# Window attention and a Fourier convolution on one core: the first rows' order, an earlier residual load, one block of transposes and a DMA queue in program order

## The chip, the cores and the metric

The kernel runs on one core of a Trainium2 chip. The metric is the device time of one execution in microseconds (us). Five engines matter: TensorE (PE, its weight loads PEld), VectorE (DVE), ScalarE (ACT), GpSimd (POOL) and SyncE (SP), which here does nothing but issue DMAs, one after the other, each with its waits.

## The reference

The input is x, 32 images of 56 x 56 tokens with 128 channels, in float32. Two residual layers follow each other:

```python
x = x + window_attention(group_norm(x))
x = x + fourier_feedforward(group_norm(x))
```

The group norm takes 32 groups of four channels over a whole image. The attention shifts the image by three, cuts it into 64 windows of 7 x 7 tokens, computes q, k and v, adds a relative position bias and a shift mask to the scores, takes the softmax of four heads, multiplies by v and projects. The second layer takes a cosine transform along the width and one along the height, keeps 32 modes of each, multiplies each mode by its own 128 x 128 matrix, transforms back, adds the two results, and applies `relu(h @ W1 + b1) @ W2 + b2` with 512 hidden channels.

## The kernel before

**Rows and cycles.** An image is worked on in eight rows of eight windows. The loop at L1006 runs over cycles; a cycle begins one row of attention and carries older work along: row `cycle` of attention gets q, k, scores and v, row `cycle - 2` (or in even cycles rows `cycle - 2` and `cycle - 1`) is transposed, row `cycle - 3` gets its product with v and its projection, and the sums for the second group norm follow a cycle later. The convolution of an image follows 11 cycles behind its attention, in steps c = 0 to 15: c = 0 the transform along the width (L645 with `dct_w`), c = 1 and 2 the one along the height (L645 with `dct_h`, from token columns "htok" that are read back from DRAM), c = 3 to 5 the mode products (`mix`, L679), which are written to DRAM ("zscr", L689), c = 5 to 8 the transform back (L718, from "zT", read from DRAM at L700), and in c = 8, 9, 10, 12, 13, 14, 15 seven groups of tokens of the feed-forward part. So a cycle of a middle image does a row of attention, a step of the convolution of the image before and often a group of the feed-forward part of the one before that.

**The order.** On PE, ACT, DVE and POOL instructions run in the order in which the Python code emits them: the whole loop stands under `manual_schedule` with these four engines (L999). SP isn't among them: the scheduler places the DMAs in its queue. Cycles 0 to 10 have no convolution and go through `first_rows` (L956); later ones go through `halves_first` (L850), `eighths`, `quarters`, `full` (L906) and `halves_last` (L927). In the last cycles, where no attention is left, a shorter sequence at L1011 to L1018 is used, which ends with `last_out`, `quarters` and `load_back`.

**PSUM.** Two sets of four banks: "pa" (`attn_bank`) for attention, "pc" (`conv_bank`) for the convolution and the feed-forward part. A bank is given out anew when its reader has finished.

**The next image.** `image_begin` (L256) starts the load of the next image's tokens "xl" in row 3, its second half follows in row 4 (`next_begin`, L947). `image_groups` (L267) turns two rows of it: fourteen transposes (L275) of a full 112 x 128 array into two banks, three copies by ACT for each pair of rows (L287, L288, L293), one `bn_stats` by DVE for each row (L297), and by POOL a memset for each row and the addition of the projection's bias to xl (L306). It is called twice in row 5 and twice in row 6; for image 1 twice in row 4 and twice in row 5 (`next_groups`, L916). Row 6 is an even cycle, and there the calls follow the attention's own transposes L474. `image_norm` (L315) then makes from the statistics the group norm's reciprocal root (L355), the scaled weights "wn" on ACT (L362), "nb" on DVE (L359) and with one small matmul of nb (L112) the bias of v, in steps that a `next(norm)` starts one by one.

**The feed-forward part.** `ff_in` (L738) first loads the residual tokens "res" (L744, L748) from DRAM, adds b2 to them on POOL (L751), and then does the four L112 products with relu on ACT (L763). `ff_out` (L766) does the second product, adds res on DVE (L787) and writes the result (L799 to L807). "res" has two buffers.

**The start.** `bias_and_mask` (L187) fills the sum of position bias and mask with sixteen small DVE additions (L193) for each of two kinds of rows; the second kind is filled in cycle 1. The second group norm's statistics come from `attn_sums` (L557): two DVE sums (L561, L570) and a square on ACT (L569), and from `fourier_stats` (L579), which ends in a reciprocal root on POOL (L616).

Of the kernel before, what the change touches and what calls it, by code (L numbers as in the profile page):

```python
# [15 lines left out]
P = 128  # L16
# [19 lines left out]
JP = 64  # L36
# [12 lines left out]
def swin_fourier_kernel(  # L49
# [33 lines left out]
    def attn_bank():  # L83
        return bank("pa", 4)

    def conv_bank():
        return bank("pc", 4)
# [96 lines left out]
    nc.gpsimd.memset(bm, 0.0)  # L184
    rpb_f = rpb.rearrange("p (t u) y x -> p t u (y x)", u=2)

    def bias_and_mask(r):  # L187
        for t in range(2):
            for half in range(2):
                rows = slice(half * JP, half * JP + WT)  # L190
                for k, p0, p1 in ((0, 0, NP - half), (1, NP - half, NP)):
                    for p in range(p0, p1):
                        nc.vector.tensor_tensor(  # L193
                            bm[rows, r, t, p],
                            rpb_f[rows, t],
                            mask_sb[rows, r, k].unsqueeze(1).to_broadcast([WT, 2, WT]),
                            ALU.add,
                        )

    bias_and_mask(0)  # L200
    dct_w = const_load([TC, 2 * NM], dct, "dct_w")
    dct_h = const.tile([TC, 2 * NM], F32, tag="dct_h", name="dct_h")
    for r in range(0, TC, S):
# [63 lines left out]
    def image_groups(im, i):  # L267


        pt = [attn_bank(), attn_bank()]  # L270
        pts = [
            p[:, : n * S].rearrange("p (j r s) -> p j r s", r=n, s=WS) for p, n in zip(pt, (8, 6))
        ]
        for c in range(7):
            nc.tensor.transpose(  # L275
                pts[c // 4][:, :, 2 * (c % 4) : 2 * (c % 4) + 2],
                im.x[:, WS * i // 2 + c],
                ident_x[:, :, SS:].rearrange("p r (j s) -> p j r s", s=WS),
            )
        for k in range(2):  # L280

            im.xw[i + k] = big.tile([P, RT + JP - WT], F32, tag="xw", name="xw", bufs=10)
            nc.gpsimd.memset(im.xw[i + k][:, RT:], 0.0)
            xw = im.xw[i + k][:, :RT]
            dst = xw.rearrange("p (j r s) -> p j r s", r=WS, s=WS)
            if k:
                nc.scalar.copy(dst[:, :, 0], pts[0][:, :, WS])  # L287
                nc.scalar.copy(  # L288
                    dst[:, :, 1:].rearrange("p j r s -> p j (r s)"),
                    pts[1].rearrange("p j r s -> p j (r s)"),  # L290
                )
            else:
                nc.scalar.copy(  # L293
                    dst.rearrange("p j r s -> p j (r s)"),
                    pts[0][:, :, :WS].rearrange("p j r s -> p j (r s)"),
                )
            nc.vector.bn_stats(im.st[:, i + k], xw)  # L297
        if im.b:
            image_bias(im, i)
# [15 lines left out]
    def image_norm(im):  # L315
# [38 lines left out]
        rstd = small.tile([P, 1], F32, tag="rstd0", name="rstd0")  # L354
        nc.gpsimd.tensor_tensor(rstd, ve, mhalf, ALU.pow)  # L355
        im.w = work.tile([P, 3 * C], F32, tag="wn", name="wn")
        yield
        nb = small.tile([P, 1], F32, tag="nb0", name="nb0")
        nc.vector.scalar_tensor_tensor(  # L359
# [3 lines left out]
        yield  # L363
        pb = attn_bank()
        halved(pb[:, 0:1], wqkv[:, 2 * C :], nb)
        im.bias = small.tile([P, 5], F32, tag="bqkv", name="bqkv")
        nc.vector.tensor_copy(im.bias[:, 2:3], pb[:, 0:1])
        yield

# [83 lines left out]
    def attn_exp(r):  # L453
        a3 = a_sb[r % 3].rearrange("p t w j -> p (t w) j")[:, :, 0:WT]
        nc.scalar.activation(a3, a3, AF.Exp)  # L455
# [279 lines left out]

    def ff_in(im, g):  # L738
        t0, n = sum(FF_GROUPS[:g]), FF_GROUPS[g]
        k, last = n // P, n % P  # L740
        xff = im.xf.rearrange("p r w -> p (r w)")
        scr_tok = im.scr.rearrange("h w c -> (h w) c")
        res = work.tile([P, 4, C], F32, tag="res", name="res")
        nc.sync.dma_start(  # L744
            res[:, :k], scr_tok[t0 : t0 + k * P].rearrange("(n p) c -> p n c", p=P)
        )
        if last:
            nc.sync.dma_start(res[:last, k], scr_tok[t0 + k * P : t0 + n])  # L748
        for c0, c1, m in ((0, k, P), (k, k + 1, last)):
            if m:  # L750
                nc.gpsimd.tensor_tensor(  # L751
                    res[:m, c0:c1],
                    res[:m, c0:c1],
                    b2sb[:m].unsqueeze(1).to_broadcast([m, c1 - c0, C]),
                    ALU.add,
                )
        im.res = res
        im.hid = []
        for f in range(NF):
            ph = conv_bank()  # L760
            halved(ph[:, :n], wff1[:, f * P : (f + 1) * P], xff[:, t0 : t0 + n])
            hf = work.tile([P, HB], F32, tag="hid", name="hid", bufs=NF)
            nc.scalar.activation(hf[:, :n], ph[:, :n], AF.Relu, bias=b1sb[:, f : f + 1])  # L763
            im.hid.append(hf)

    def ff_out(im, g):  # L766
        t0, n = sum(FF_GROUPS[:g]), FF_GROUPS[g]
# [67 lines left out]
    def load_back(cycle):  # L835
        for im, c in fourier(cycle):
            for width, g in back_groups(c):
                load_modes(im, width, g)

    def nothing():  # L840
        while True:
            yield
# [7 lines left out]
    def halves_first(cycle, norm):  # L850
# [8 lines left out]
        im, i = row(cycle)  # L859
        if im:  # L860
            attn_qk(im, i, False)
        next(norm)
        next(sums)
        for im, c in fourier(cycle):
            if c in FF_AT:
# [1 line left out]
        for im, c in fourier(cycle):  # L867
            if c == 0:
                next(im.stats)

    def has_ff(cycle):
        return any(c in FF_AT for _, c in fourier(cycle))
# [43 lines left out]
    def next_groups(cycle):  # L916
        b, i = divmod(cycle, NWR)
        if b + 1 < NB:
            for j in {(4 if b == 0 else 5): (0, 2), (5 if b == 0 else 6): (4, 6)}.get(i, ()):
                image_groups(images[b + 1], j)  # L920

    def last_out(cycle):
# [4 lines left out]
    def halves_last(cycle, norm):  # L927
# [6 lines left out]
        load_back(cycle + 1)  # L934
        next_begin(cycle)
        load_first(cycle)
        next(norm)
        if row(cycle)[0]:
            attn_exp(cycle)
            attn_divide(cycle)  # L940
# [1 line left out]
        if im:  # L942
            last_out(cycle)
            attn_project(im, j)
        next(norm)

    def next_begin(cycle):  # L947
        b, i = divmod(cycle, NWR)
# [7 lines left out]
    def first_rows(cycle, norm):  # L956
# [15 lines left out]
            attn_max(cycle)  # L972
        if im3:
            attn_project(im3, i3)
        next(norm)
        last, j = row(cycle - 4)
        if last:
            for _ in attn_sums(last, j):
# [2 lines left out]
            attn_v(im, i, cycle)  # L981
        if cycle < NWR // 2:
            image_bias(im, 2 * cycle)
        if cycle == 1:
            bias_and_mask(1)
        next(norm)
        next_begin(cycle)
        next_groups(cycle)
        if cycle == CONV_BEGIN - 1:
            attn_exp(cycle)  # L990
            attn_divide(cycle)
            for _ in attn_sums(im3, i3):
                pass
            last, j = row(cycle - 1)
            attn_transpose(last, j, cycle - 1)
        next(norm)

    ET = mybir.EngineType
    with tc.manual_schedule(engines={ET.PE, ET.Activation, ET.DVE, ET.Pool}):  # L999
        images[0] = image_begin(0)  # L1000
        for i in range(0, NWR, 2):
            image_groups(images[0], i)
        for _ in image_norm(images[0]):
            pass
        norm = nothing()
        for cycle in range(NB * NWR + CONV_BEGIN + FF_AT[-1] - NWR + 1):  # L1006
            if cycle < CONV_BEGIN:
                first_rows(cycle, norm)
# [16 lines left out]
                full(cycle)  # L1025
                halves_last(cycle, norm)
            b, i = divmod(cycle, NWR)
            norm = nothing()
            if i == (NWR - 2 if b else NWR - 3) and b + 1 < NB:
                norm = image_norm(images[b + 1])  # L1030
                next(norm)


# [60 lines left out]
```

## Time and profile before

| | |
|---|---|
| time, median of three runs | 3634.03 us (3633.53 to 3636.36) |
| profiled execution | 3641.7 us, span 3639.9 us |
| granted TensorE clock, mean | 0.995 |
| instructions | 161,666 |
| DMA | 390.31 MB, 107 GB/s on average |

Three groups of the profile's fifth part show the largest shares of TensorE: L112 from "hid" (12,544 matmuls of 128 x 128, 740.3 us), L112 from "xf" (3,584 matmuls, 717.5 us) and L112 from "xw" (2,048 matmuls, 390.6 us). The transposes L275 are 896 of 72,192 matmuls. How to read it: each line of that part is a group of equal instructions with its engine, source line, what it writes and reads, count, busy time, mean duration and the idle time of its engine just before it. A "128*64" is the part of the array that a matmul uses. L112 is a helper that splits every product into two halves of 64 columns, so that line is told apart by its tiles. The waits, the timeline and the stretches shown below are answers of the same trace.

### The profile page before, as it was taken

Reading aid. Unit: us, or ns where it says so; the run is one execution under the profiler, and the core shown is the slowest. Engines: PE = TensorE matmul, PEld = TensorE weight load, DVE = VectorE, ACT = ScalarE, POOL = GpSimd, SP = SyncE. Lnnn points to the kernel's source line nnn. Section 1 sums busy time; section 2 is a strip of 40 time slices with the busy share of each in tenths; the row PEclk is TensorE's granted clock in tenths of the full one; section 3 lists DMA queues with packets and bytes.
Section 4 is the critical chain, followed back from the end, with each engine's and each line's share of the span. In section 5 each row is a group of like instructions: output and inputs, shape, how many; then the busy total and the mean of one; then the engine's idle time right before and its main releaser. Section 6 shows DMA issues by size and latency. Waiting matters only on the chain.

```text
span 3639.9 us, 161666 instructions
## 1 busy us (share of the span) xinstructions
PE 3574.4 (98%) x72192; PEld 2832.6 (78%) x72192; DVE 2211.9 (61%) x4738; ACT 2148.1 (59%) x4044; POOL 1368.3 (38%) x1421
## 2 busy tenths in 40 slices
PE   7899999999999999999999999999999999999999
PEld 5677777778777787877777878777777777787776
DVE  7766666666666666666656656666566666565641
ACT  4555566655566555666556665556665556655553
POOL 5433333333343433333333434333333334343321
PEclk8999999999999999999999999999999999999999
DMA  4334434444434444334444344443444443444343
GB/s 114 86 102 112 113 96 111 108 110 111 112 97 112 112 109 116 94 110 107 113 108 111 94 114 109 113 114 94 111 108 111 110 111 94 114 109 109 97 115 98
DMA packets 687350, 390.31 MB, mean 107 GB/s; under 512 B 39967, under 2 KB 657600, under 8 KB 686400
## 3 DMA queue, kind: packets, MB, share of 16 engines
q1 hardware_dynamic: 686045, 379.65, 38.3%
q8 instruction: 568, 9.31, 1.1%
q14 instruction: 126, 1.03, 0.1%
q10 hardware_dynamic: 611, 0.32, 0.0%
HBM read 218.29 MB, written 161.48 MB: 104 GB/s over the span
## 4 chain that ended last, share of the span: by engine, by line
PE 92%; DVE 4%; issue 1%; ACT 1%; POOL 1%; DMA 1%; SPq 0%; POOLq 0%; DVEq 0%; ACTq 0%
PE pc L112 37%; PE pa L112 14%; PE pa L408 6%; PE pc L679 6%; PE pa L474 6%; PE pc L645 6%; PE pa L430 5%; PE pa L499 4%; PE pc L718 4%; PE pa L275 3%; DVE a L438 1%; DVE xf L729 0%; DVE oT L530 0%; POOL rstd L616 0%; ACT a L455 0%
## 5 line engine op out<-in xcount | busy, mean ns | idle before, releaser
L449 POOL TENSOR_TENSOR a<-a,mx 128x784 f32<-128x784 f32 x256 | 389.4, 1521 | 1427.3 <-DVE mx L448 1203.4
L112 PE MATMUL pc<-wff,hid 128*64 128x128 f32 x12544 | 740.3, 273 | 1.5 <-ACT hid L763 0.8
L112 PE MATMUL pc<-xf,wff 128*64 128x512 f32 (+2 forms) x3584 | 717.5, 539 | 1.1 <-DVE xf L729 1.0
L112 PEld LDWEIGHTS pc<-wff,hid 128*64 128x64 f32 x12544 | 702.6, 137 | 8.2 <-ACT hid L763 4.5
L460 DVE TENSOR_REDUCE sm<-a 128x16 f32<-128x784 f32 x256 | 248.2, 970 | 686.1 <-ACT a L455 682.8
L463 POOL TENSOR_TENSOR a<-a,rs 128x784 f32<-128x784 f32 x256 | 389.1, 1520 | 566.6 <-DVE rs L462 542.8
L763 ACT ACTIVATE hid<-pc,b1sb 128x512 f32<-128x512 f32 (+2 forms) x896 | 527.1, 632 | 76.6 <-PE pc L112 74.5
L112 PEld LDWEIGHTS pc<-xf,wff 128*64 128x64 f32 x3584 | 279.8, 137 | 368.0 <-issue 260.5
L379 ACT ACTIVATE q<-pa,bqkv 128x392 f32<-128x392 f32 x256 | 150.4, 587 | 473.1 <-PE pa L112 467.5
L112 PE MATMUL pa<-xw,wn 128*64 128x392 f32 (+1 forms) x2048 | 390.6, 497 | 3.7 <-DVE aT L484 2.7
L530 DVE TENSOR_SCALAR oT<-pa,bqkv 128x98 f32<-128x98 f32 (+2 forms) x768 | 171.0, 278 | 268.7 <-PE pa L499 268.6
L751 POOL TENSOR_TENSOR res<-res,b2sb 128x512 f32<-128x512 f32 (+2 forms) x256 | 264.2, 1037 | 113.5 <-DMA res<-scr 113.5
L408 PE MATMUL pa<-wn,xw 128*64 128x128 f32 x4096 | 283.6, 280 | 4.7 <-issue 3.5
L306 POOL TENSOR_TENSOR xl<-xl,bproj 112x512 f32<-112x512 f32 (+1 forms) x256 | 286.8, 1142 | 0.0
L499 PEld LDWEIGHTS pa<-aT,v 49*32 49x32 f32 x16384 | 172.9, 106 | 146.1 <-issue 127.0
L415 ACT COPY v<-pa 128x512 f32<-128x512 f32 x256 | 150.9, 589 | 228.3 <-PE pa L408 228.3
L438 DVE TENSOR_TENSOR a<-pa,bm 128x392 f32<-128x392 f32 x512 | 264.8, 559 | 25.8 <-PE pa L430 2.1
L455 ACT ACTIVATE a<-a 128x784 f32<-128x784 f32 x256 | 222.3, 869 | 97.2 <-POOL a L449 96.8
L482 ACT COPY aT<-pa 113x452 f32<-113x452 f32 x256 | 139.4, 544 | 210.4 <-PE pa L474 206.6
L408 PEld LDWEIGHTS pa<-wn,xw 128*64 128x64 f32 x4096 | 221.4, 137 | 38.6 <-issue 9.1
L112 PE MATMUL pa<-wproj,oT 128*64 128x128 f32 (+1 forms) x3584 | 248.0, 274 | 1.8 <-DVE oT L530 1.8
L448 DVE TENSOR_REDUCE mx<-a 128x16 f32<-128x784 f32 x256 | 246.3, 962 | 4.3
(91 smaller groups left out, 5583.8 us busy)
## 6 DMA issues: line engine op xcount, KB each, us to landing
zscr<-z SPq DMA_DIRECT2D x512, 112.0 KB
htok<-scr SPq DMA_DIRECT2D x256, 196.0 KB
zT<-zscr SPq DMA_DIRECT2D x192, 256.0 KB
res<-scr SPq DMA_DIRECT2D x160, 256.0 KB
out_dram<-res SPq DMA_DIRECT2D x160, 256.0 KB
scr<-xl SPq DMA_DIRECT2D x128, 224.0 KB
xl<-in_x_dram SPq DMA_DIRECT2D x32, 784.0 KB
xl<-in_x_dram SPq DMA_DIRECT2D x32, 672.0 KB
```

The lines of the kernel that those rows point to most:

```text
L112: nc.tensor.matmul(dst[ps], lhsT=lhsT[:, ps], rhs=rhs, start=start, stop=stop)
L306: nc.gpsimd.tensor_tensor(piece, piece, bproj.unsqueeze(1).to_broadcast([TC, e - a, C]), ALU.add)
L408: nc.tensor.matmul(pv[hs, j * C : (j + 1) * C], lhsT=im.xw[i][:, w * WT : w * WT + JP], rhs=im.w[:, 2 * C : 3 * C], start=True, stop=True,)
L438: nc.vector.tensor_tensor(a[:, 2 * hp : 2 * hp + 2, :, 0:WT].rearrange("p u w j -> p w u j"), ps[hp][:, :RT].rearrange("p (w u j) -> p w u ...
L448: nc.vector.tensor_reduce(mx, a3, axis=AX.X, op=ALU.max)
L449: nc.gpsimd.tensor_tensor(a3, a3, mx.unsqueeze(2).to_broadcast([P, 2 * NWR, WT]), ALU.subtract)
L455: nc.scalar.activation(a3, a3, AF.Exp)
L460: nc.vector.tensor_reduce(sm, a3, axis=AX.X, op=ALU.add)
L463: nc.gpsimd.tensor_tensor(a3, a3, rs.unsqueeze(2).to_broadcast([P, 2 * NWR, WT]), ALU.mult)
L499: nc.tensor.matmul(po4[u][h * HD : (h + 1) * HD, 2 * f + e], lhsT=v[ks, 2 * f + e, h * HD : (h + 1) * HD], rhs=im.aT[i][f][ks, h, e * JP : ...
L751: nc.gpsimd.tensor_tensor(res[:m, c0:c1], res[:m, c0:c1], b2sb[:m].unsqueeze(1).to_broadcast([m, c1 - c0, C]), ALU.add,)
L763: nc.scalar.activation(hf[:, :n], ph[:, :n], AF.Relu, bias=b1sb[:, f : f + 1])
```

## The change

It has these parts:

- `bias_and_mask` is cut into four parts of four L193 each; for the second kind of rows part 0 is emitted in cycle 1, part 1 in cycle 2, parts 2 and 3 in cycle 3, instead of all in cycle 1.
- `image_groups` takes "pc" banks for rows 2 and 6, "pa" banks for rows 0 and 4; from the second image on all four calls stand in row 6, instead of two in row 5 and two in row 6.
- The norm of image 0 runs three steps ahead of the loop, and its last step (the matmul of nb) after the first scores. That of image 1 does its statistics in cycle 6 and the rest in cycle 7, instead of all in cycle 6.
- In cycle 10 the sums of row 7 stand ahead of the exponential and the division of the last row.
- The residual is loaded by `load_residual` at the end of the cycle before, after that cycle's `load_modes`; the addition of b2 on POOL stands after the feed-forward products and after `fourier_stats`.
- SP is added to the engines of `manual_schedule`.

```diff
-    def bias_and_mask(r):
-        for t in range(2):
-            for half in range(2):
...
+    def bias_and_mask(r, part):
+
+        t, half = divmod(part, 2)
...
-        pt = [attn_bank(), attn_bank()]
+
+        pt = [conv_bank() if i % 4 else attn_bank() for _ in range(2)]
...
-    def ff_in(im, g):
+    def load_residual(im, g):
...
+        im.next_res = res
...
+    def ff_residual(im, g):
...
             for width, g in back_groups(c):
                 load_modes(im, width, g)
+            if c in FF_AT:
+                load_residual(im, FF_AT.index(c))
...
         for im, c in fourier(cycle):
             if c == 0:
                 next(im.stats)
+        for im, c in fourier(cycle):
+            if c in FF_AT:
+                ff_residual(im, FF_AT.index(c))
...
-            for j in {(4 if b == 0 else 5): (0, 2), (5 if b == 0 else 6): (4, 6)}.get(i, ()):
+            for j in ({4: (0, 2), 5: (4, 6)} if b == 0 else {6: (0, 2, 4, 6)}).get(i, ()):
...
-        if cycle == 1:
-            bias_and_mask(1)
-        next(norm)
+        for part in {1: (0,), 2: (1,), 3: (2, 3)}.get(cycle, ()):
+            bias_and_mask(1, part)
+        if cycle == NWR - 1:
+            next(norm, None)
         next_begin(cycle)
         next_groups(cycle)
         if cycle == CONV_BEGIN - 1:
+            for _ in attn_sums(im3, i3):
+                pass
             attn_exp(cycle)
             attn_divide(cycle)
-            for _ in attn_sums(im3, i3):
-                pass
...
-        next(norm)
...
-    with tc.manual_schedule(engines={ET.PE, ET.Activation, ET.DVE, ET.Pool}):
+    with tc.manual_schedule(engines={ET.PE, ET.Activation, ET.DVE, ET.Pool, ET.SP}):
...
-        for _ in image_norm(images[0]):
-            pass
-        norm = nothing()
+        norm = image_norm(images[0])
+        for _ in range(3):
+            next(norm)
```

On each engine the same instructions are issued as before, in another order; half of the L275 transposes write to the other set of banks. In the built SP queue, against the one of before, a middle image shows these moves: the first half of the next image's xl stands ahead of the first four htok loads instead of behind them, and the second half comes a cycle later; the zT loads of L718's first and second cycles stand behind the zscr writes of the same cycle instead of ahead of them; every residual load stands near the end of the cycle before its use, instead of wherever the scheduler put it. At the very end the last residual load stands behind the last but one group's output instead of ahead of it.

## The prediction

> **What bounds the kernel now.** I read the page first: the busy line, the 40 slices and the chain that ended last.
>
> ```profile
> PE 3574.4 (98%) x72192; PEld 2832.6 (78%) x72192; DVE 2211.9 (61%) x4738; ACT 2148.1 (59%) x4044; POOL 1368.3 (38%) x1421
> ...
> PE   7899999999999999999999999999999999999999
> ...
> PE 92%; DVE 4%; issue 1%; ACT 1%; POOL 1%; DMA 1%; SPq 0%; POOLq 0%; DVEq 0%; ACTq 0%
> ```
>
> TensorE is busy 98% and holds 92% of the chain; only its first slices are below nine tenths. An edit off TensorE can therefore pay only in the first 200 us or at the end; elsewhere it must shorten TensorE's own sequence. The stretches say the same (busy time of PE, PEld, DVE, ACT, POOL; granted clock; DMA share; GB/s):
>
> ```profile
> 40.00:72.00 32.00, 30.35 (x587) 22.96 (x589) 27.34 (x57) 20.03 (x42) 26.63 (x29) 0.89 0.71 222
> 72.00:84.00 12.00, 7.59 (x126) 5.07 (x126) 7.14 (x23) 5.12 (x9) 2.64 (x3) 0.67 0.08 20
> ...
> 1000.00:1110.70 110.70, 110.51 (x2258) 88.36 (x2257) 68.77 (x148) 66.83 (x126) 42.60 (x44) 1.00 0.40 109
> ```
>
> An image in the middle costs 110.70 us with 0.2 us of visible idling; 72 to 84 us is half empty and at two thirds of the clock. Then the timeline of TensorE around the next image's transposes (start, length, line), first in an odd cycle, then in the even one after it, and from the waits what stops the second (total, times, longest):
>
> ```profile
> 1013.39 0.91 PE L430 MATMUL pa<-k,q 64*64 64x98 f32 x32
> 1014.23 1.72 PE L275 MATMUL pa<-ident_x,xl 112*128 112x112 f32 x14
> 1015.88 1.09 PE L408 MATMUL pa<-wn,xw 128*64 128x128 f32 x16
> ...
> 1027.33 1.85 PE L474 MATMUL pa<-ident,a 113*113 113x113 f32 x16
> 1029.01 1.98 PE L275 MATMUL pa<-ident_x,xl 112*128 112x112 f32 x14
> 1030.92 1.09 PE L408 MATMUL pa<-wn,xw 128*64 128x128 f32 x16
> ```
>
> ```profile
> PEld pa L275 <- DVE aT L484: 7.6, 29, 0.3
> ```
>
> From first start to the next line's start, the odd block takes 1.65 us and the even one 1.91 us. The even one stops once for 0.3 us, because its second pair of "pa" banks is the pair that L484 still copies from. Last, the start-up's DVE and TensorE, and SP's queue:
>
> ```profile
> 33.69 6.23 DVE L193 TENSOR_TENSOR bm<-rpb,mask 49x98 f32<-49x98 f32 x16
> ...
> 77.12 0.38 PE L112 MATMUL pa<-nb,wqkv 128*64 128x1 f32 x4 [4.41 <-DVE nb L359]
> ...
> 1055.17 1.13 SPq L700 DMA_DIRECT2D zT<-zscr  x2
> 1060.18 1.63 SPq L689 DMA_DIRECT2D zscr<-z  x4
> ...
> 1093.94 1.79 SPq L667 DMA_DIRECT2D htok<-scr  x4
> 1099.54 2.00 SPq L118 DMA_DIRECT2D xl<-in_x_dram  x2
> ```
>
> **What the Trainium skill says.** "TensorEngine Tiling (Array Packing)", section Key Properties: changing the tiling mode drains TensorE. The trace agrees: inside a block the transposes start 0.102 us apart, but the first takes 0.156 and the last, before the 64-column L408, 0.192. "TensorE: Matmul & The Clock Gate", What's actually happening: an idle window of about 3.4 us halves the clock. It agrees: after the 4.41 us wait the eight L112 matmuls of cycle 7 take 2.8 us, against 1.4 us in cycle 8. "SBUF — State Buffer", Who interferes with whom: a DVE instruction with two SBUF inputs is blocked by a GpSimd one that reads SBUF. It agrees: L193 has two, takes 0.25 us alone, but three of the sixteen took 1.57, 1.32 and 0.97 us beside L449 and L306. "DMA: Bandwidth & Descriptors", Queues, rings and completion order: an engine consumes its descriptors in ring order, so a load waits out what was queued ahead of it; this trace has only consistent cases.
>
> **The change, part by part** (minus is time saved).
>
> *One transpose block.* The same 28 transposes are issued per image, all in the cycle after L474. The odd block's 1.65 us goes; 14 more transposes cost 14 x 0.102 = 1.43. So one entry and one exit go (0.05 + 0.09), and with them the 0.3 us wait: between the first pair of "pa" banks and the second now stand seven transposes (0.7 us) into "pc", so L484 is done. I take one extra bank-change step of 0.055: 1.65 + 1.43 + 0.055 = 3.14 against 1.65 + 1.91 = 3.56. Saved 0.41 an image, between 0.25 (a 0.15 us bank wait stays) and 0.52. Images 3 to 31 are TensorE-bound: 29 x 0.41 = **-11.9** (-7 to -15). What comes with the block hides. ACT's twelve copies take about 0.9 us a group, so its row is 3.6 us long, and it idles 40%. DVE's eight L297 end before the row's exp does. POOL gets eight L306 (8 x 1.14 = 9.1 us) ahead of L463, which then ends some 5 us later, but its reader L474 comes over a cycle (13 us) later; behind it wait L355 and L751, whose readers also have a cycle.
>
> *Norm of image 1 over cycles 6 and 7.* TensorE no longer waits for nb. DVE then paces: its L460 rows are 13.2 us apart (69.58 to 82.79) over that wait, and 8.0 in the half-clock cycle after it, against 6.5 in undisturbed cycles. The norm's own DVE work is 2.6 + 0.3. Saved (13.2 + 8.0) - (2 x 6.5 + 2.9) = 5.3, and 0.2 for the missing wake-up: **-5.5** (-4 to -6.5).
>
> *Bias of L193 in thirds.* Four now stand ahead of L484 instead of sixteen; the fourth ended at 36.84, the last at 39.92, so 3.1 us earlier. The other twelve move behind L448 and L547 of cycles 2 and 3, beside L449 and the two L306, where each POOL instruction blocks one: about 1.8 and 2.3 us given back, as DVE paces those cycles. **+1** (-2 to +3).
>
> *Sums ahead of exp in cycle 10.* They fill 1.08 us in which DVE waits for L455, less the wait for the square: **-0.6** (-1.2 to 0). *nb's matmul after the first scores, eight banks for image 0:* 0, since L112 waits for wn (ready 18.38) and the second half of the transposes for its DMA (10.5).
>
> *SP in program order.* (a) The next image's xl goes ahead of htok. In a middle image SP stands at xl until L645 ends and issues it at 1099.54, as now; htok, and behind it out and scr, come after; 784 + 784 KB at 233 KB/us (191 GB/s at a DMA share of 0.82 in 1104 to 1112 us) plus 1.7 us of latency (res, 128 KB: issued 3630.07, used 3632.32) lands near 1108; L645 needs it at 1112.6: 0. In image 0 nothing stands before L645: xl at 118.8, htok's first group lands near 125.5, needed at 123.1, and the second group adds a little; the cycle has a 2.1 us wait of its own behind it. **+2.5** (0 to +3.5). (b) zT for L718's second cycle goes from 1055.2 to behind L689 and the residual: issued until 1063.5, landed by 1063.5 + 1.7 + 384/233 = 1066.9, needed at 1069.6: 0. That for its first cycle lands 4 us early, the later two are held by the zT buffers as now. (c) The residual a cycle ahead waits for an out DMA issued a cycle before: 0. POOL's reciprocal root L616 stands before L751 now; no middle image waited on it: 0. (d) At the end the last residual goes behind the last but one out DMA (3632.96 + 0.49): issued 3633.5, added by 3636.5, where L787 now starts at 3635.73: **+0.8** (0 to +1.5).
>
> Sum: -11.9 - 5.5 + 1 - 0.6 + 2.5 + 0.8 = -13.7. The span of the profiled execution, 3639.9, would become 3626.2. The three timed runs stand at 3633.5 to 3636.4, median 3634.03, 5.9 under that span; the same cut gives **3620 us**.
>
> **The rivals.** *R1, the blocks don't pack:* every seven transposes wait for a bank and 28 cost what two blocks cost. For it: each block shows one or two 0.156 steps. Against it: eight banks are in turn, and ACT frees a group in 0.9 us. 3620 + 12 = 3632. *R2, the irregular waits change:* images 3 to 30 take 111.24 us on average against the smallest 110.70, together 15 us, most of it ended by "issue" at L408, L718 and L645 while DMA bursts run. The new order spreads xl's second half to a later cycle; half of it gone is 3612, all 3605; half as much again is 3628. *R3, slower:* L718's second cycle waits for zT each image, since it is now queued behind 448 KB of L689 and 160 KB of residual. The gain is used up when it lands 0.5 us after 1069.6, that is 6.6 us after its last issue, where I count 3.4; a forecast of slower by 0.2% needs 0.7 us after; 1 us an image gives 3620 + 29 = 3649. Against it: the DMA engines are 23% busy from 1059 to 1065. That the change doesn't do what it says can't be: the built order shows one block of 28.
>
> **How the numbers follow.** My forecast 0.58 (alone 3612 to 3629: ends of the start-up terms and of the block), R1 0.12, R2 down 0.14, R2 up 0.08, R3 0.08. Within 0.2% (7.3 us, about what this kernel's measurement can tell from no change) lie most of R1, half of R2 up and the upper tail of the forecast: 0.20; slower is R3, 0.08; faster the rest, 0.72. The range 3606 to 3634 leaves out R3 and the far ends.
>
> **What would show it.** One L275 group of 28 of about 3.14 us between L474 and L408, and L430 to L408 directly in the odd cycle; a smallest image of 110.3; no wait on nb near 77 us; a wait at L645 near 123 us; L787 at the end waiting for the residual. Wrong if the image period stays at 110.7, if L718 waits at its second cycle, or if the start-up, measured to the first middle image, isn't shorter by 1 to 5 us.

## The result, and the profile after

The changed kernel takes 3654.23 us (median of four runs, 3651.56 to 3654.81), the kernel before, in runs beside it, 3635.2 us (median of four, 3633.53 to 3639.87). The ratio is 1.0049, with a 95% interval of 1.0031 to 1.0066: slower by about 19 us between the medians, where 3620 was predicted, with 3634 as the upper end of the range. The profiled execution of the changed kernel took 3651.56 us, its span is 3649.7 us, 9.8 more than the span before (3639.9).

Lines of the changed file stand a little lower, and those of the runs differ again by a few. Here L408 is now L410, L430 L432, L474 L476, L275 L277, L438 L440, L448 L450, L530 L532, L645 L647, L718 L720, L729 (the transform's sum into xf on DVE) L731, L616 and L618 (root and shift) L618 and L620, L359 (nb) L362, L787 L798, and the residual's addition on POOL, L751, is L770.

From the page, the busy line, TensorE's slices and the chain that ended last:

```profile
PE 3557.7 (97%) x72192; PEld 2824.6 (77%) x72192; DVE 2291.8 (63%) x4738; ACT 2146.0 (59%) x4044; POOL 1370.7 (38%) x1421
...
PE   6899999999999999999999999999999999999999
...
PE 82%; DVE 10%; issue 3%; POOL 3%; ACT 1%; DMA 1%; SPq 0%; POOLq 0%; DVEq 0%; ACTq 0%
```

TensorE's busy time fell by 16.7 us, as a shorter block of transposes should make it. But its share of the chain fell from 92% to 82%, and DVE's went from 4% to 10%: something on DVE now sets the time again and again. DVE itself is busy 80 us longer with the same work, so some of its instructions take longer. The three stretches are two in the start and one image in the middle. Their columns are length, busy time of PE, PEld, DVE, ACT and POOL, granted clock, DMA share and GB/s:

```profile
40.00:72.00 32.00, 26.65 (x536) 20.33 (x536) 31.05 (x60) 19.25 (x41) 24.16 (x28) 0.89 0.62 202
72.00:84.00 12.00, 8.91 (x200) 6.85 (x200) 11.21 (x30) 6.18 (x12) 6.67 (x6) 1.00 0.08 21
1000.00:1111.18 111.18, 110.17 (x2258) 87.88 (x2256) 71.39 (x148) 66.83 (x126) 42.63 (x45) 1.00 0.41 108
```

A middle image takes 111.18 us, 0.48 more than before, and DVE is busy 2.6 us more in it. TensorE's timeline around the transposes (start, length, line) shows that this isn't their doing:

```profile
1031.95 0.91 PE L432 MATMUL pa<-k,q 64*64 64x98 f32 x32
1032.78 1.85 PE L476 MATMUL pa<-ident,a 113*113 113x113 f32 x16
1034.47 0.93 PE L277 MATMUL pa<-ident_x,xl 112*128 112x112 f32 x7
1035.23 0.88 PE L277 MATMUL pc<-ident_x,xl 112*128 112x112 f32 x7
1035.94 0.87 PE L277 MATMUL pa<-ident_x,xl 112*128 112x112 f32 x7
1036.65 0.87 PE L277 MATMUL pc<-ident_x,xl 112*128 112x112 f32 x7
1037.46 1.09 PE L410 MATMUL pa<-wn,xw 128*64 128x128 f32 x16
```

From the first start to L410 the 28 transposes take 2.99 us, where 3.14 was predicted and 3.56 stood before. So 0.57 us an image were won there, and as the image is 0.49 longer, about 1.06 were lost elsewhere. The waits of TensorE from 300 to 3600 us (total, times, longest) show where, first in the kernel after, then in the one before:

```profile
PE pc L647 <- DVE xf L731: 30.9, 29, 1.2
```

```profile
PE pc L645 <- DVE xf L729: 0.2, 1, 0.2
```

Once in each of 29 images the first transform along the width waits for DVE's sum into xf. The timeline of POOL, DVE and TensorE around one of these waits, in the kernel after (start, length):

```profile
1099.60 0.55 POOL L618 TENSOR_TENSOR rstd<-ve,mhalf 128x1 f32<-128x1 f32 x1 [3.04 <-DVE ve L614]
1100.11 1.27 POOL L770 TENSOR_TENSOR res<-res,b2sb 128x512 f32<-128x512 f32 x1
...
1100.18 1.22 DVE L620 SCALAR_TENSOR_TENSOR shift<-ms,rstd 128x1 f32<-128x1 f32 x1 [0.66 <-POOL rstd L618]
1101.32 0.66 DVE L532 TENSOR_SCALAR oT<-pa,bqkv 128x98 f32<-128x98 f32 x3
1101.90 1.02 DVE L440 TENSOR_TENSOR a<-pa,bm 128x392 f32<-128x392 f32 x2
1102.85 1.73 DVE L731 TENSOR_TENSOR xf<-pc,xf 128x448 f32<-128x448 f32 x4
...
1103.51 1.21 PE L647 MATMUL pc<-dct_w,xl 112*64 112x64 f32 x34 [1.01 <-DVE xf L731]
```

And the same place in the kernel before:

```profile
1093.07 0.55 POOL L616 TENSOR_TENSOR rstd<-ve,mhalf 128x1 f32<-128x1 f32 x1 [1.81 <-DVE ve L612]
...
1093.65 0.16 DVE L618 SCALAR_TENSOR_TENSOR shift<-ms,rstd 128x1 f32<-128x1 f32 x1 [0.66 <-POOL rstd L616]
1093.72 0.67 DVE L530 TENSOR_SCALAR oT<-pa,bqkv 128x98 f32<-128x98 f32 x3
1094.31 1.03 DVE L438 TENSOR_TENSOR a<-pa,bm 128x392 f32<-128x392 f32 x2
1095.25 1.74 DVE L729 TENSOR_TENSOR xf<-pc,xf 128x448 f32<-128x448 f32 x4
```

The shift, one number per partition, takes 1.22 us instead of 0.16 and ends with the residual's addition, which POOL began 0.07 us before it. Everything behind it on DVE comes 1.06 us later, and L647 reuses a "pc" bank that L731 empties. In the trace after, 31 of the 32 shifts start while L770 runs, and those take 1.216 to 1.232 us; the one of the first image, which has no feed-forward part beside it, takes 0.159. In the kernel before, L751 ran from 1089.97 to 1091.25, 2.4 us ahead of the shift; 31 of its 32 shifts take 0.16 us, and only the last image's, which meets an addition, takes 1.27.

The start also went another way than predicted: forecast 2.6 us shorter in all, it became 3.5 longer. TensorE's and DVE's timelines after:

```profile
85.00 0.38 PE L112 MATMUL pa<-nb,wqkv 128*64 128x1 f32 x4 [2.83 <-DVE nb L362]
85.21 2.89 PE L112 MATMUL pa<-xw,wn 128*64 128x393 f32 x8
...
126.20 3.25 PE L647 MATMUL pc<-dct_h,htok 112*64 112x64 f32 x56 [4.20 <-DMA htok<-scr]
...
34.26 3.15 DVE L193 TENSOR_TENSOR bm<-rpb,mask 49x98 f32<-49x98 f32 x4
41.11 3.97 DVE L193 TENSOR_TENSOR bm<-rpb,mask 49x98 f32<-49x98 f32 x4
50.01 4.58 DVE L193 TENSOR_TENSOR bm<-rpb,mask 49x98 f32<-49x98 f32 x8
```

The wait on nb is still there, only later. L647 waits 4.20 us for htok; that wait was foreseen. The sixteen L193 take 11.7 us, where 6.23 stood before. The start is counted up to the middle images, that is to v's product (L410) of the fourth image's first row, "image 3" in the prediction, which counts from 0. It is 285.1 us, against 281.6 before.

An image's time is counted from its first v's product to that of the next image. The shortest of 27 such times is called the smallest image, and what the 27 take together above 27 times the smallest are the irregular waits. The sum over the two traces is then: start +3.5; 27 images at 0.49 more in the smallest, +13.3; irregular waits 15.2 before and 6.4 after, -8.8; the rows of the last two images +1.4; from the last row's L410 to the end +0.5. That is +9.9, of the 9.8 in the spans.

### The profile page after: what moved, and what is told of

It reads as the page before. It is cut to its first block, busy times and chain, and to the rows that moved or that the text cites. A ratio compares the mean times of both kernels' runs of the same rounds, so it can differ in the third digit from the quotient of the medians.

```text
span 3649.7 us, 161663 instructions
## 1 busy us (share of the span) xinstructions
PE 3557.7 (97%) x72192; PEld 2824.6 (77%) x72192; DVE 2291.8 (63%) x4738; ACT 2146.0 (59%) x4044; POOL 1370.7 (38%) x1421
## 4 chain that ended last, share of the span: by engine, by line
PE 82%; DVE 10%; issue 3%; POOL 3%; ACT 1%; DMA 1%; SPq 0%; POOLq 0%; DVEq 0%; ACTq 0%
PE pc L112 33%; PE pa L112 12%; PE pc L681 6%; PE pc L647 6%; PE pa L410 5%; PE pa L432 5%; PE pa L476 5%; PE pa L501 4%; PE pc L720 3%; DVE xf L731 2%; DVE a L440 2%; POOL a L451 1%; PE pa L277 1%; PE pc L277 1%; POOL a L465 1%
## 5 line engine op out<-in xcount | busy, mean ns | idle before, releaser
L451 POOL TENSOR_TENSOR a<-a,mx 128x784 f32<-128x784 f32 x256 | 389.4, 1521 | 1281.1 <-DVE mx L450 879.8
L465 POOL TENSOR_TENSOR a<-a,rs 128x784 f32<-128x784 f32 x256 | 389.1, 1520 | 613.9 <-DVE rs L464 537.3
L770 POOL TENSOR_TENSOR res<-res,b2sb 128x512 f32<-128x512 f32 (+2 forms) x256 | 264.0, 1036 | 220.1 <-DMA res<-scr 172.8
L532 DVE TENSOR_SCALAR oT<-pa,bqkv 128x98 f32<-128x98 f32 (+2 forms) x768 | 170.9, 277 | 252.6 <-PE pa L501 252.4
L410 PE MATMUL pa<-wn,xw 128*64 128x128 f32 x4096 | 284.2, 280 | 4.7 <-issue 2.2
L308 POOL TENSOR_TENSOR xl<-xl,bproj 112x512 f32<-112x512 f32 (+1 forms) x256 | 287.0, 1143 | 0.0
L440 DVE TENSOR_TENSOR a<-pa,bm 128x392 f32<-128x392 f32 x512 | 264.8, 559 | 24.9 <-PE pa L432 0.8
L798 DVE TENSOR_TENSOR res<-pc,res 128x512 f32<-128x512 f32 (+3 forms) x257 | 139.2, 550 | 180.2 <-PE pc L112 136.5
L432 PE MATMUL pa<-k,q 64*64 64x98 f32 x8192 | 235.9, 251 | 15.4 <-DVE k L398 5.7
L410 PEld LDWEIGHTS pa<-wn,xw 128*64 128x64 f32 x4096 | 221.9, 137 | 37.5 <-issue 4.1
```

The source lines that it names most:

```text
L308: nc.gpsimd.tensor_tensor(piece, piece, bproj.unsqueeze(1).to_broadcast([TC, e - a, C]), ALU.add)
L410: nc.tensor.matmul(pv[hs, j * C : (j + 1) * C], lhsT=im.xw[i][:, w * WT : w * WT + JP], rhs=im.w[:, 2 * C : 3 * C], start=True, stop=True,)
L432: nc.tensor.matmul(ps[hp][HALVES[e], pr * 2 * WT : (pr + 1) * 2 * WT], lhsT=q[cs, w * WT : w * WT + JP], rhs=k_sb[cs, :, w], start=True, s ...
L440: nc.vector.tensor_tensor(a[:, 2 * hp : 2 * hp + 2, :, 0:WT].rearrange("p u w j -> p w u j"), ps[hp][:, :RT].rearrange("p (w u j) -> p w u ...
L451: nc.gpsimd.tensor_tensor(a3, a3, mx.unsqueeze(2).to_broadcast([P, 2 * NWR, WT]), ALU.subtract)
L465: nc.gpsimd.tensor_tensor(a3, a3, rs.unsqueeze(2).to_broadcast([P, 2 * NWR, WT]), ALU.mult)
```

## The experiments

The theory (theory 1): **the port.** POOL's addition and DVE's shift want the same read interface of SBUF; moved behind the root, the addition gets it first and holds it for its whole length (the lock, below). "SBUF — State Buffer" in the Trainium skill, section Who interferes with whom, says that a DVE instruction with two SBUF inputs contends with a GpSimd one that reads SBUF, since its second input comes through a shared interface; the shift has two (ms and rstd). The rivals: the new SP order or the early load brings the wait (theory 2); the transposes in the "pc" banks bring it (theory 3); or the root's result reaches DVE late (theory 4).

| run | median us | ratio to before (95%) | smallest image | start of middle images |
|---|---|---|---|---|
| before | 3635.2 | 1 | 110.69 | 281.6 |
| after | 3654.23 | 1.0049 (1.0031 to 1.0066) | 111.18 | 285.1 |
| 1, additions back ahead of the root | 3625.14 | 0.996 (0.9947 to 0.9972) | 110.12 | 286.1 |
| 2, before, additions behind the root | 3664.14 | 1.0064 (1.005 to 1.0078) | 111.77 | 279.4 |
| 3, shift with one input | 3628.87 | 0.9966 (0.9954 to 0.9979) | 110.18 | 287.6 |
| 4, before, one block of transposes | 3626.86 | 0.9961 (0.9948 to 0.9973) | 110.13 | 282.3 |
| 5, as 1, SP left to the scheduler | 3623.61 | 0.9965 (0.9951 to 0.9978) | 110.11 | 279.7 |
| 6, as 1, htok ahead of xl | 3623.69 | 0.9966 (0.9954 to 0.9978) | 110.11 | 285.1 |
| 7, as 1, nb earlier | 3621.30 | 0.9957 (0.9944 to 0.9971) | 110.12 | 283.1 |
| 8, as 1, L193 in one cycle | 3623.01 | 0.9962 (0.9948 to 0.9976) | 110.12 | 282.7 |
| 9, as 1, with 6, 7 and 8 | 3618.24 | 0.994 (0.9928 to 0.9953) | 110.11 | 278.2 |
| 10, as 9, SP left to the scheduler | 3621.67 | 0.9947 (0.9935 to 0.996) | 110.11 | 275.7 |
| 11, as 9, third image's transposes in two cycles | 3618.64 | 0.9937 (0.9924 to 0.9951) | 110.11 | 273.5 |

The kernel before had medians of 3639.71 us beside runs 1 to 4, 3636.86 beside 5 to 8 and 3640.36 beside 9 to 11, so the ratios are what is compared. All the intervals leave out 1. The last two columns are taken from each run's one trace, at the starts of v's product. A start is good to about 2 us: runs with the same instructions up to there differ by that much already at 60 us.

**1. The additions put back.**

```diff
         for im, c in fourier(cycle):
+            if c in FF_AT:
+                ff_residual(im, FF_AT.index(c))
+        for im, c in fourier(cycle):
             if c == 0:
                 next(im.stats)
-        for im, c in fourier(cycle):
-            if c in FF_AT:
-                ff_residual(im, FF_AT.index(c))
```

> The changed kernel with one thing put back: POOL's residual adds stand ahead of the reciprocal root again (ff_residual called before the second step of the spectral statistics); the residual is still loaded a cycle early, and SP's queue stays as the change has it. Theory 1 (the residual add, now right behind the root on POOL, holds the shared SBUF port while VectorE's shift with its two SBUF inputs wants it): the shift takes about 0.16 us again instead of 1.22, PE's wait at the first height transform for the xf sum is gone, the interval from qk of row 3 to qk of row 4 falls from 17.97 to about 16.90 us, the smallest image from 111.18 to about 110.1, and the time from 3654 by 29 x 1.06 = 31 us to about 3623. Theory 2 (the wait comes from SP's new order or the early load) and theory 3 (it comes from the 28 transposes in the pc banks): the wait of 1.0 us in every image stays, and so does the time, 3654 within 4 us.

The run takes 3625.14 us, against 3623 expected. The waits of TensorE from 300 to 3600 us, and DVE's timeline of that run:

```profile
PE pc L647 <- DVE xf L731: 1.2, 8, 0.2
```

```profile
1094.11 0.16 DVE L620 SCALAR_TENSOR_TENSOR shift<-ms,rstd 128x1 f32<-128x1 f32 x1 [0.66 <-POOL rstd L618]
```

The waiting went from 30.9 us to 1.2, the shift is 0.16 us again, and the interval between v's products of rows 3 and 4 is 16.91 us (17.97 after). Theories 2 and 3 are out: the queue, the early load and the "pc" banks are all still there.

**2. The additions moved in the kernel before.**

```diff
+    def ff_residual(im, g):
...
         for c0, c1, m in ((0, k, P), (k, k + 1, last)):
...
             if c == 0:
                 next(im.stats)
+        for im, c in fourier(cycle):
+            if c in FF_AT:
+                ff_residual(im, FF_AT.index(c))
```

> The kernel before with one thing of the change: POOL's residual adds moved behind the reciprocal root; the load stays where it was and SP's queue is left to the scheduler. Theory 1: the shift takes about 1.2 us, PE waits about 1.0 us for xf in every image, the smallest image goes from 110.70 to about 111.8, and the time from 3635 by 31 us to about 3666. Theories 2 and 3: nothing of that, 3635 within 4 us.

The run takes 3664.14 us, against 3666 expected. From its waits and its timeline:

```profile
PE pc L645 <- DVE xf L729: 29.9, 27, 1.2
```

```profile
1097.95 1.27 POOL L764 TENSOR_TENSOR res<-res,b2sb 128x512 f32<-128x512 f32 x1
...
1098.02 1.22 DVE L618 SCALAR_TENSOR_TENSOR shift<-ms,rstd 128x1 f32<-128x1 f32 x1 [0.66 <-POOL rstd L616]
```

One move in the old kernel brings the whole loss, 0.64%, and a smallest image 1.08 us longer. The median stands 24 us above that of the kernel before, not 31. In the two traces the irregular waits were 8.0 us here and 15.2 before, which is of the right size for the rest.

**3. The shift with one tensor input.**

```diff
-        nc.vector.scalar_tensor_tensor(
-            out=shift, in0=ms[:, 0:1], scalar=-SQRT_S, in1=rstd, op0=ALU.mult, op1=ALU.mult
-        )
+        nc.vector.tensor_scalar(shift, ms[:, 0:1], rstd, -SQRT_S, ALU.mult, ALU.mult)
```

> The changed kernel, order untouched, with the shift written as one tensor input (the mean) times a per-partition scalar (the root) times a constant, in place of two tensor inputs. Theory 1, if a per-partition scalar doesn't count as a second SBUF input: the shift takes under 0.3 us beside the running add, and the time falls to about 3623. Theory 1, if the scalar counts as one too: the shift still takes 1.2 us and the time stays at 3654. Theory 4 (not the port: the root's own result reaches VectorE only when POOL goes on): the shift still starts late or takes 1.2 us, 3654.

The run takes 3628.87 us, against 3623 expected, with the order of the changed kernel untouched. Two lines of its timelines, and TensorE's wait for the sum into xf (L729 here):

```profile
1096.00 1.28 POOL L768 TENSOR_TENSOR res<-res,b2sb 128x512 f32<-128x512 f32 x1
...
1096.07 0.21 DVE L620 TENSOR_SCALAR shift<-ms,rstd 128x1 f32<-128x1 f32 x1 [0.66 <-POOL rstd L618]
...
PE pc L645 <- DVE xf L729: 4.6, 23, 0.2
```

The addition starts 0.07 us ahead of the shift, as in the kernel after, and the shift passes it in 0.21 us; 31 of 32 do (0.212 to 0.216), and the one with nothing beside it takes 0.214 too. Theory 4 is out: rstd reaches DVE at the same time (0.66 us of waiting in both). A late addition by itself costs nothing either, since it is as late here. What held the shift was its form with two tensor inputs. The edit changes the instruction along with the operand, so the two aren't told apart; both forms read the same two numbers from SBUF. The new form is 0.05 us longer than 0.16, and TensorE then waits for xf in 23 images, up to 0.2 us: this chain has no room at all.

**4. The block alone.**

```diff
-        pt = [attn_bank(), attn_bank()]
+        pt = [conv_bank() if i % 4 else attn_bank() for _ in range(2)]
...
-            for j in {(4 if b == 0 else 5): (0, 2), (5 if b == 0 else 6): (4, 6)}.get(i, ()):
+            for j in ({4: (0, 2), 5: (4, 6)} if b == 0 else {6: (0, 2, 4, 6)}).get(i, ()):
```

> The kernel before with the one block of 28 transposes alone (its second pairs in the pc banks, all four groups in the seventh row's cycle). Theory 1: the block takes 2.99 us in place of 1.65 + 1.91, so 0.58 x 28 = 16 us less: the smallest image about 110.1, the time about 3619. Theory 3 (the transposes in the pc banks bring the wait at the first height transform): a wait of 1.0 us per image shows there and the time goes to about 3635 - 16 + 30 = 3649.

The run takes 3626.86 us, a ratio of 0.9961: about 14 us less by the ratio, 16 expected, and the smallest image 0.56 shorter. So theory 3 is out from this side too. This is practically all that the change has to give in a middle image: with every other part of it, in run 1, the smallest is 110.12, against 110.13 here.

**5 and 6. The queue.** In run 5 `ET.SP` is taken out of `manual_schedule` again; in run 6 it stays, and two calls change places:

```diff
+        load_first(cycle)
         next_begin(cycle)
-        load_first(cycle)
```

> The run with the residual adds put back ahead of the root (3625), with one more part of the change undone: SP's DMA queue is left to the scheduler again, so that the column loads of a new image stand ahead of the load of the image after it. If the queue in program order is what costs at the start (PE's wait of 4.4 us for the column tokens at 123 us) and what saves the irregular waits in the middle (9.7 us over 27 images there against 15.3 in the run with one block alone): the wait at 123 us shrinks by 2 to 4 us, the irregular waits go back to about 15, and the time ends at 3625 + 5 - 2 = 3628. If the irregular waits have nothing to do with the queue: 3623.

> The run with the residual adds put back (3625), with the two column loads of a new image issued ahead of the image load in the same cycle, SP else in program order. If the queue order causes the wait at 123 us: the cycle before the second image's fifth row falls from 13.99 us to about 11.9, the start of the middle images from 286 to about 284, nothing changes in a middle image (smallest 110.13), time about 3623. Rival: the column loads wait for what is written to scr, not for the queue: 13.99 and 3625 stay.

Neither time can be told from run 1's. Without the program order the middle images do start earlier in the traces: 6.4 us in run 5 against run 1, 2.5 in run 10 against run 9 below. Of that, 4.1 and 1.8 stand there already at cycle 11's v, ahead of the wait for htok, and 2.3 and 0.7 come behind it. How much of the first part is the queue's isn't shown. In run 6 the wait for htok is gone, but the stages behind it give the gain back; its TensorE timeline:

```profile
123.17 1.95 PE L647 MATMUL pc<-dct_h,htok 112*64 112x64 f32 x56
125.06 1.05 PE L501 MATMUL pa<-aT,v 49*32 49x49 f32 x64
127.73 0.91 PE L432 MATMUL pa<-k,q 64*64 64x98 f32 x32 [1.63 <-DVE k L398]
```

L647 starts at 123.17 instead of 128.27 (run 1), 5.1 us earlier; but then TensorE waits for DVE's k, later for more, and 1.0 us is left at the fourth image. The queue order does cause that wait, and most of what its removal gains is lost again in waits of the cycles behind it. The irregular waits were 9.8 us in run 1 and 12.2 in run 5. Over all traces of the study they lie between 6.4 and 13.1 with the queue in program order and between 8.0 and 15.3 without: what ends them is not settled. They are smallest, 6.4 and 8.0, in the two traces in which every image waits for xf.

**7. nb ahead of the row's sums.**

```diff
+        if cycle == NWR - 1:
+            next(norm, None)
         if cycle:
             attn_divide(cycle - 1)
...
-        if cycle == NWR - 1:
-            next(norm, None)
```

> The run with the residual adds put back (3625), with one more edit: in the last row of the first image the second image's nb (two SBUF inputs on VectorE) is put ahead of the row's sums, while POOL is idle, in place of behind the projection's add, where POOL subtracts maxima; the matmul on it then stands ahead of the row's v. Theory (the norm of the second image spread over two cycles gains little since nb lands at 86.7 us, queued behind the row's VectorE work and held 1.1 us by POOL's subtraction): the gap of 2.84 us before the matmul on nb goes, the first qk of the second image takes 1.5 in place of 2.9 us, the cycle falls from 11.37 to about 8 us, time about 3622. Rival: VectorE paces these cycles, so what PE gains there it waits for at the next scores: the second image's rows start no more than 1 us earlier, 3625.

The run takes 3621.30 us. First why nb is late in the kernel after (timelines of DVE and POOL), then TensorE in this run:

```profile
83.57 1.29 DVE L362 SCALAR_TENSOR_TENSOR nb<-back,rstd 128x1 f32<-128x1 f32 x1
...
83.33 1.51 POOL L451 TENSOR_TENSOR a<-a,mx 128x784 f32<-128x784 f32 x1 [0.45 <-DVE mx L450]
```

```profile
83.23 0.23 PE L112 MATMUL pa<-nb,wqkv 128*64 128x1 f32 x4
83.81 1.09 PE L410 MATMUL pa<-wn,xw 128*64 128x128 f32 x16 [0.34 <-DVE a L440]
84.73 1.74 PE L112 MATMUL pa<-xw,wn 128*64 128x393 f32 x8
```

nb has two SBUF inputs and was held by L451 exactly as the shift by L770. Ahead of the sums it takes 0.15 us, the 2.8 us wait goes, and from cycle 7's v to cycle 8's pass 7.1 us instead of 11.4 (run 1). At the fourth image 3.0 us of it are left, 3.8 when both traces are counted from cycle 7's v. So the rival, all given back, doesn't fit these traces; the times alone, 3621.30 against run 1's 3625.14, don't decide it, since the intervals overlap.

**8. The mask in one cycle.**

```diff
-        for part in {1: (0,), 2: (1,), 3: (2, 3)}.get(cycle, ()):
+        for part in {1: (0, 1, 2, 3)}.get(cycle, ()):
             bias_and_mask(1, part)
```

> The run with the residual adds put back (3625), with the 16 bias-and-mask adds of the last row all in the second row's cycle again, as before the change. If the eight adds put into the fourth row's cycle lie on the path (they take 1.05 to 1.58 us each beside POOL): that cycle falls from 9.42 to about 6.8 us, the second and third grow by about 0.5 each, and the middle images start 1.5 to 2 us earlier, 3623. Rival: VectorE paces all of these cycles and only the sum counts: no change at the fifth row's start (58.4 us) within 0.5, 3625.

The run takes 3623.01 us, which can't be told from run 1's. From cycle 3's v to cycle 4's pass 6.9 us instead of 9.4 (run 1), and 3.4 us are left at the fourth image, in traces whose starts differ by up to 2 us anyhow. DVE's timeline has the sixteen at their old price, where the thirds took 11.7 us:

```profile
34.87 6.23 DVE L193 TENSOR_TENSOR bm<-rpb,mask 49x98 f32<-49x98 f32 x16
```

**9 to 11. Together.** Run 9 has the edits of 1, 6, 7 and 8; run 10 takes SP out of it; run 11 splits the third image's transposes:

```diff
-            for j in ({4: (0, 2), 5: (4, 6)} if b == 0 else {6: (0, 2, 4, 6)}).get(i, ()):
+            for j in ({4: (0, 2), 5: (4, 6)} if b == 0 else {5: (0, 2), 6: (4, 6)} if b == 1 else {6: (0, 2, 4, 6)}).get(i, ()):
```

> The changed kernel with four mends together: the residual adds ahead of the root, the mask adds of the last row in one cycle, the second image's nb ahead of the row's sums, the column loads ahead of the image load. Each alone, on top of the first, moved the start of the middle images from 286.1 to 282.7 (mask), 283.1 (nb) and 285.1 (columns). If they add up: 286.1 - 3.4 - 3.0 - 1.0 = 278.7, and the time 3625 - 7 = 3618, 0.55% under before. If VectorE paces these cycles and the gains are the same slack counted twice: about 282, 3622.

> As the run with four mends, with SP's DMA queue left to the scheduler. If the queue in program order is worth nothing either way (so far 3623.6 against 3625.1 without mends): the same time as the run with four mends within 2 us, 3618. If it costs at the start what the run without mends showed (279.7 in place of 286.1 at the start of the middle images): about 275 there and 3614. If the order saves irregular waits: 3622.

> As the run with four mends, with the transposes of the third image (made while the first rows of the second still run at VectorE's pace) split over two cycles again as before the change. The one block put 16.1 us where 11 stood before in the seventh cycle of that image and took 2 off the sixth, net about 1.5 at the start of the middle images. If so: 278.7 - 1.3 = 277.4, 3617. Rival: VectorE's own work is the same in both, and the next cycles give it back: within 0.5 of the run with four mends.

Run 9 gives 3618.24 us, 0.6% under the kernel before; its middle images start at 278.2, expected 278.7, so within those 2 us the gains add up. From its page:

```profile
PE 3558.4 (98%) x72192; PEld 2831.4 (78%) x72192; DVE 2255.8 (62%) x4738; ACT 2147.3 (59%) x4044; POOL 1372.0 (38%) x1421
...
PE 93%; DVE 4%; ACT 1%; POOL 1%; issue 1%; DMA 0%; SPq 0%; POOLq 0%; DVEq 0%; ACTq 0%
```

TensorE's busy time is that of the kernel after, 3558; its share of the chain is 93% again. In run 11 the stretch from cycle 11's v (near 114 us) to the fourth image is 159.6 us instead of 163.6, so the split is worth some 4 us in that trace, where 1.3 was expected; its time isn't below run 9's by anything that these runs can tell. Run 10's middle images start at 275.7 us, expected 275, but its time, 3621.67, isn't below run 9's either: 3614 was expected with that start.

## Why the prediction was wrong

**The step that failed** is in the part on SP's order, under (c): "POOL's reciprocal root L616 stands before L751 now; no middle image waited on it: 0." TensorE didn't wait on the root itself, but DVE did, in every image of the trace before:

```profile
DVE shift L618 <- POOL rstd L616: 21.2, 32, 0.7
```

So the shift always starts just as the root ends, and what POOL begins then starts beside it. The prediction didn't ask that. The addition had run while DVE did other things; put behind the root it starts 0.07 us ahead of the shift. The skill's page stood in the prediction, for L193, and what it says holds for L620 too: 1.22 us beside the addition, 0.16 without. Runs 1, 2 and 3 show the cause from three sides. Price: 1.06 us x 29 images = 31 us, against a predicted gain of 13.7. Between run 1 and the kernel after lie 0.0089 in the ratio, 32 us. Without this step the change comes out as run 1, about 14 us faster, next to the forecast of 13.7. That is partly luck: in its trace the start is 4.5 us longer where 2.6 less was forecast, and a larger gain of the block and irregular waits of 9.8 us, for which no gain was counted, made up for it.

Two of the prediction's own signs of being wrong came: the smallest image went up instead of to 110.3, and the start wasn't shorter.

*R3* had the right form, a new wait of 1 us an image, at another place: from 300 to 3600 us TensorE's L720 never waited for zT. That its 3649 lies near the measured 3654 is chance.

*One block.* Right in kind, mis-sized: 0.57 us saved an image, not 0.41. I charged an extra bank step of 0.055 and kept the inner steps; in the trace the inner groups of seven start 0.71 us apart, 7 x 0.102, so changing banks costs nothing there. (A call of `image_groups` makes seven transposes, not fourteen, four into one bank and three into another.) In the trace before, too, the changes of bank without a wait show steps of 0.10; the steps of 0.156 inside the two blocks stand behind weight loads that came 0.1 to 0.3 us late, and the new block has none of these. *R1* is out. But the third image's block falls into cycles of the start, and there it isn't free: some 4 us in run 11's trace. The prediction had no term for it.

*Norm of image 1, -5.5.* "TensorE no longer waits for nb" failed: the wait moved from 77 to 85 us. From cycle 6's v to cycle 8's passed 19.0 us instead of 21.3, so 2.3 were won. With run 7's edit it is 15.2, that is 6.0 won: the predicted gain was there, behind the same lock.

*L193 in thirds, +1.* It was priced with the lock, at 4.1 us given back over two cycles. As foreseen, three L193 were held in each of them, but two of the four in cycle 1 were held as well; in all the thirds cost 5.5 us more of DVE, and about 3 us of time (run 8's trace), the upper end of the term.

*Queue, +2.5 for image 0.* The wait came, at 4.20 us; 1.0 us of it stays by run 6's trace, 0.7 and 2.3 by those of runs 10 and 5. Middle images: 0, as predicted. *The end, +0.8:* L798 does wait for the residual there, and from the last row's L410 to the end pass 153.2 to 153.6 us in all eight traces with SP in program order, 152.2 to 152.7 in the five without: about +1.0. *Sums in cycle 10, -0.6:* no run of its own; not shown.

*R2:* the irregular waits fell from 15.2 to 6.4 us in the profiled pair. The spans differ by 9.8 us and the medians by 19, since the profiled execution of before was 6.5 us above its median and that of after 2.7 below; whether the irregular waits make that difference isn't shown.

## What to carry to other kernels

When a step on POOL moves, look at what DVE will run during it, not only at who waits for its result: a DVE instruction of 0.16 us with two SBUF inputs can cost as much as the POOL instruction beside it, and in a chain between two engines' banks TensorE pays for it. Order the long POOL work ahead of a short result that DVE answers at once, or write that one number with one tensor and a per-partition scalar. A start-up that DVE paces and a middle that TensorE paces have to be costed apart: there a freed wait may be given back (run 6 kept 1.0 of 5.1 us in its trace) or mostly kept (run 7: 3.0 of 4.2), and here every 0.5 us counts 29 times.

## What was not expected of the hardware

- A `tensor_scalar` of one number per partition, with one tensor and a scalar read from SBUF, isn't held by a POOL instruction that reads SBUF: 0.212 to 0.216 us in 31 meetings, against 1.216 to 1.232 for the form with two tensors. A `tensor_scalar` of 32 numbers is held: the norm's L326 and, right behind it, L341 with two tensors, in the kernel after (timelines of DVE and POOL):

```profile
1045.67 0.55 DVE L326 TENSOR_SCALAR gmeans<-gsums 128x32 f32<-128x32 f32 x1
1046.25 1.45 DVE L341 TENSOR_TENSOR turned<-turned,gmeans 128x32 f32<-128x32 f32 x1
...
1043.93 2.25 POOL L308 TENSOR_TENSOR xl<-xl,bproj 112x512 f32<-112x512 f32 x2
1046.13 1.53 POOL L465 TENSOR_TENSOR a<-a,rs 128x784 f32<-128x784 f32 x1
```

L326 ends about 0.04 us after the second L308 and takes 0.55 us instead of 0.18; L341 waits out L465, 1.45 instead of 0.19. Both came with the one block, which queues eight L308 there: run 4 has them, run 2 hasn't. Over the kernel that is 10.8 and 36.5 us of DVE, and with the shift's 31.8 it makes up nearly all of the 80 us. But the norm's part costs no time that shows: with it run 4 has a smallest image of 110.13, 0.56 less than before, where the transposes alone save 0.57. The same lock costs 31 us where TensorE waits behind DVE, and nothing a cycle later.

- In the kernel after, TensorE's clock halved after a shorter pause than the idle window of about 3.4 us that "TensorE: Matmul & The Clock Gate" in the Trainium skill, section What's actually happening, gives: 2.83 us, from 82.17 to 85.00 (two stretches of one us around its end):

```profile
84.00:85.00 1.00, 0.00 (x0) 0.03 (x1) 1.00 (x2) 0.00 (x0) 0.84 (x1) 0.89 0.35 90
85.00:86.00 1.00, 1.00 (x8) 0.61 (x10) 1.00 (x3) 0.00 (x0) 0.00 (x0) 0.50 0.32 90
```

The granted clock goes from 1.00 to 0.50 just before work resumes, and the eight products behind it take 2.89 us, where those of the cycles before and after take 1.49. In run 7, where the pause is gone, the clock stays at 1.00 there and the eight take 1.74. So this wait costs some 1.2 to 1.4 us more than it shows.
